# Moving the transposition and the broadcast of the attention maxima later in a block of queries

## The chip, the core and the metric

The kernel runs on one core of a Trainium2 chip. The core has a matrix engine (TensorE, PE in the profile; its weight loads are PEld), a vector engine (VectorE, DVE), a scalar engine (ScalarE, ACT), a general engine (GpSimd, POOL) and an engine that only issues transfers (SyncE, SP). They run side by side, each through its own list of instructions in a fixed order, and wait for one another by semaphores. The metric is the device time of one execution in microseconds (us). Everything is computed in float32.

## What is computed

Four layers run over `x` of shape 4 x 64 x 64 x 128 (four images of 4096 positions with 128 channels). Layer 0 is attention over 7 x 7 neighbourhoods. Layer 1, in which the change lies, is full attention of every position over all 4096 positions of its image:

```python
h = group_norm(x, gn_scale, gn_bias)
hf = h.reshape(B, N, C)                      # N = 4096, C = 128
q = hf @ wq + bq
k = hf @ wk + bk
v = hf @ wv + bv
w_ = jnp.einsum('bqd,bkd->bqk', q, k) * C ** (-0.5)
w_ = jax.nn.softmax(w_, axis=2)
o = jnp.einsum('bqk,bkd->bqd', w_, v)
o = o @ wo + bo
return x + o.reshape(B, H, W, C)
```

Layer 2 is a gated linear layer with a layer norm, four tiles of 128 positions at a time. Layer 3 is a selective scan with a depthwise 3 x 3 convolution ahead of it.

## The kernel before

The kernel goes image by image (`b` of 4). For each image `layer_1` works through 32 blocks of 128 queries, `i`. A block's scores against the 4096 keys are computed with the keys on the partitions: 32 tiles of 128 keys, four of which make a group (`G = 4`, eight groups, `g`). The softmax of a block is spread over three turns of the loop, so that TensorE always has products of two blocks to mix:

- In turn `i` (`score`, L607 to L620), each group is four products into one PSUM tile (L613, `sc`). ScalarE copies the tile into `st` in SBUF (L616), which holds all 32 tiles of scores. VectorE keeps an elementwise maximum over the key tiles in `mx`: one instruction after group 3 (L618) and one each after groups 5 and 7 (L620).
- At the start of turn `i + 1`, `fold` (L622 to L625) halves `mx` three times, to one maximum per partition of keys and per query. During that turn `soften` (L627 to L640) finishes the maximum and takes the exponential. TensorE transposes the 128 x 128 maxima (L630, `pt`), VectorE reduces them to one negative maximum per query (L632, `nm`) and spreads these on a diagonal (L634, `dm`), and TensorE multiplies the diagonal by ones (L636, `pb`), which brings each query's maximum to all partitions. VectorE adds `pb` to the scores in two halves (L639), and ScalarE takes the exponential of each half in place (L640).
- In turn `i + 2`, `value` (L642 to L646) multiplies each key tile of exponentials by the values; a column of ones beside the values gives the sum. `finish` (L648 to L651) divides and adds to `x`, which lies in `xt`.

Within a turn the program says, for each group: soften the block before if it is its place, then four scores of block `i`, then four value products of block `i - 2`. `soften` has its place ahead of the scores of group 2; after the last block, where there are no scores, at group 0.

After each turn `between(i)` does a piece of other work: a step of layer 2 for the positions that are done, and a piece of the front of layer 3 (`front`) for positions that went through layer 2. Layer 2 has four steps, one per turn, in a cycle of four: `turn` (transposes, L275, and a sum, L689), `mix` (L695 to L710), `add` (L717 to L727) and `norm` (four normalising instructions on VectorE, L734, a transposition and L742). The front of layer 3 puts in projections (L786, L814), the convolution's taps (L828, L843 and L847 on ScalarE, L855 and L858 on GpSimd, L864 on VectorE), activations (L806) and small products (L914, L919, L935, L940, L947).

The program order isn't the order on the engines. A scheduler decides, ahead of the run, the order of each engine's list: it goes by the program order as a priority and by its own estimate of when each instruction is ready, and it may let an instruction stand behind later ones of the program. The semaphores follow from the order. Only a few instructions are kept in program order explicitly (L806 among them).

Buffers around the change: four PSUM tiles are shared by the scores and the products of layers 2 and 3 (tag "s"), two by `pt`, `pb` and other transpositions (tag "t"), two by `po` and others (tag "o"). `st` is in a ring of five large SBUF tiles, `mx1` and `dm1` have two buffers each, `nm1` three.

Of the kernel before, what the change touches and what calls it, by code (L numbers as in the profile page):

```python
# [22 lines left out]
F32 = mybir.dt.float32  # L23
AF = mybir.ActivationFunctionType
ALU = mybir.AluOpType
# [4 lines left out]
P = 128  # L30
B, H, W, C = 4, 64, 64, 128
L = H * W
NT = L // P
# [105 lines left out]
def layers_0_to_2(  # L139
    ctx, tc, xf, mata, matb, rows, rpb, convw, sel, ident, cl, dram, big, ring, early, x3_d, ub_d, zf_d, y_d, dbl_d, ct_d, gw_d, bw_d  # L140
):
    nc = tc.nc
    wp = ctx.enter_context(tc.tile_pool(name="wa", bufs=1))
    tmp = ctx.enter_context(tc.tile_pool(name="tmp", bufs=2))
# [8 lines left out]
    def ps_t(shape, name):  # L153
        return psp.tile(shape, F32, name=name, tag="t", bufs=2)
# [90 lines left out]
    ones = wp.tile([P, P], F32, name="ones")  # L245
# [308 lines left out]
    def layer_1(b, xt, hT, st, between):  # L554
# [49 lines left out]
        def start(i):  # L604
            k = Block()
            k.st = ring([P, NT, P], "st")
            k.mx = tmp.tile([P, 2 * G, P], F32, name="mx1", tag="mx1")  # L607
            return k

        def score(i, k, g):  # L610
            ps = ps_s([P, G, P], "sc1")
            for r in range(G):
                nc.tensor.matmul(  # L613
                    ps[:, r, :], lhsT=kT[:, bass.ts(G * g + r, P)], rhs=qT[:, bass.ts(i, P)], start=True, stop=True
                )
            nc.scalar.copy(k.st[:, G * g:G * g + G, :], ps)  # L616
            if g == 3:
                nc.vector.tensor_tensor(k.mx, k.st[:, 0:8, :], k.st[:, 8:16, :], ALU.max)  # L618
            elif g in (5, 7):
                nc.vector.tensor_tensor(k.mx, k.mx, k.st[:, 4 * g - 4:4 * g + 4, :], ALU.max)  # L620

        def fold(k):  # L622
            mx = k.mx
            for n in (4, 2, 1):
                nc.vector.tensor_tensor(mx[:, 0:n, :], mx[:, 0:n, :], mx[:, n:2 * n, :], ALU.max)  # L625

        def soften(k):  # L627
            mx = k.mx
            pt = ps_t([P, P], "pt1")
            nc.tensor.transpose(pt, mx[:, 0, :], ident)  # L630
            nm = sml.tile([P, 1], F32, name="nm1", tag="nm1")
            nc.vector.tensor_reduce(nm, pt, AX.X, ALU.max, negate=True)  # L632
            dm = tmp.tile([P, P], F32, name="dm1", tag="dm1")
            nc.vector.tensor_scalar(dm, ident, nm, None, ALU.mult)  # L634
            pb = ps_t([P, P], "pb1")
            nc.tensor.matmul(pb, lhsT=ones, rhs=dm, start=True, stop=True)  # L636
            for h in range(2):
                part = k.st[:, 16 * h:16 * h + 16, :]
                nc.vector.tensor_tensor(part, part, pb.unsqueeze(1).to_broadcast([P, 16, P]), ALU.add)  # L639
                nc.scalar.activation(part, part, AF.Exp)  # L640

        def value(k, g):  # L642
            if g == 0:
                k.po = ps_o([P, C + 1], "po1")
            for j in range(G * g, G * g + G):
                nc.tensor.matmul(k.po, lhsT=k.st[:, j, :], rhs=v[:, j, :], start=(j == 0), stop=(j == NT - 1))  # L646

        def finish(i, k):  # L648
            ri = sml.tile([P, 1], F32, name="ri1", tag="ri1")
            nc.vector.reciprocal(ri, k.po[:, C:C + 1])  # L650
            nc.vector.scalar_tensor_tensor(xt[:, i, :], k.po[:, 0:C], ri, xt[:, i, :], ALU.mult, ALU.add)  # L651

        blocks = {}
        for i in range(NT + 2):
            if 0 < i <= NT:
                fold(blocks[i - 1])
            if i < NT:
                blocks[i] = start(i)
            for g in range(NT // G):

                if 0 < i <= NT and g == (2 if i < NT else 0):
                    soften(blocks[i - 1])
                if i < NT:
                    score(i, blocks[i], g)
                if i >= 2:
                    value(blocks[i - 2], g)
            if i >= 2:
                finish(i - 2, blocks.pop(i - 2))
            between(i)
# [414 lines left out]
    for b in range(B):  # L1084
# [5 lines left out]
        def between(i):  # L1090

            n, part = divmod(i - 6, 4)
            if i == 6 and b + 1 < B:
                ahead.append(load_x(b + 1))
            if i >= 6 and n < NCH:
                parts[part](n)
            first_part(i)
            if b + 1 < B and i == NT + 1:
                edge_of[b + 1] = edge_bias(0)
            if b + 1 < B and i == NT + 3:  # L1100
                bias_m[:] = bias_tiles()
                for t, d in zip(bias_m, bias_d):
                    nc.sync.dma_start(t, d)

        first_part = front(b)
        first_part(-1)
        layer_1(b, xt, *handed.pop(b), between)
        if b + 1 < B:
            coming = layer_0(b + 1, ahead[0], edge_of[b + 1])
# [379 lines left out]
```

## Time and profile before

| | |
|---|---|
| median of 3 runs | 3786.41 us (3785.8 to 3787.2) |
| the profiled execution's own time | 3789.72 us |
| its span on the core | 3787.9 us, 69412 instructions |
| layer 1 of the four images | 248 to 744, 984 to 1526, 1752 to 2290, 2516 to 3067 us of the span |
| busy in these four stretches, 2127 us | PE 2026.6, DVE 1696.2, ACT 1483.9, POOL 474.6 us |

The profile is of one execution. A line of the list of waits names the engine and line that waited, for whom, the total in us, how often, and the longest. In a list in order of time each line has a start, a length in us, the engine, the line of the kernel, the operation, what is written from what with partitions x elements, and how many such instructions stand together. In brackets is how long the engine stood idle before it, and whose signal ended that. One matrix product of the program is recorded as two instructions; so a group of four scores is "x8".

### The profile page before, as it was taken

The numbers are of one execution on the slowest core, as the hardware profiler recorded it, in microseconds if no ns is written. First come the engines' busy times: TensorE is split into PE (matmuls) and PEld (weight loads), VectorE is DVE, ScalarE is ACT, GpSimd is POOL, SyncE is SP. The second block draws the span as 40 slices with busy tenths as digits, with TensorE's granted clock in tenths as the row PEclk, the third lists the DMA queues.
The fourth block names the chain that finished last, engine by engine and source line by source line (L and its number), as shares of the span: only waits on it lengthen the run. The fifth ranks groups of instructions, "written<-read, shape, count | busy, mean of one in ns | idle before, by whom it ended". The sixth has DMA issues, their size and how long they took to land.

```text
span 3787.9 us, 69412 instructions
## 1 busy us (share of the span) xinstructions
PE 3375.8 (89%) x26780; PEld 2780.8 (73%) x26780; DVE 2838.1 (75%) x4865; ACT 2679.2 (71%) x4350; POOL 1421.5 (38%) x1562
## 2 busy tenths in 40 slices
PE   6999999999999999998999999989999987666647
PEld 3779989966789889667998897779988863222236
DVE  2657777766677788666777876767778866999968
ACT  3865667778677776686676777867767657999934
POOL 5500012245122122351212223523222226999866
PEclk8999999999999999999999999999999996555569
DMA  5100000131010012310211113100101158999998
GB/s 139 50 3 26 12 18 29 44 100 35 18 46 29 32 64 89 118 41 12 71 60 64 46 43 97 44 1 26 44 27 62 54 192 207 232 223 206 210 273 287
DMA packets 205199, 319.30 MB, mean 84 GB/s; under 512 B 23583, under 2 KB 112188, under 8 KB 200732
## 3 DMA queue, kind: packets, MB, share of 16 engines
q1 hardware_dynamic: 165572, 237.57, 18.4%
q0 software_dynamic: 19776, 68.56, 9.9%
q10 hardware_dynamic: 19520, 8.73, 0.8%
q8 instruction: 211, 3.46, 0.4%
q14 instruction: 120, 0.98, 0.1%
HBM read 150.91 MB, written 155.56 MB: 81 GB/s over the span
## 4 chain that ended last, share of the span: by engine, by line
PE 54%; DVE 22%; POOL 8%; ACT 7%; issue 6%; DMA 3%; SPq 1%; POOLq 0%; DVEq 0%; ACTq 0%
PE po L646 15%; PE sc L613 15%; DVE mx L625 4%; POOL inp L1216 4%; PE pt L493 4%; DVE acc L864 4%; DVE st L639 3%; DVE mx L620 3%; POOL y L1255 2%; PE po L504 2%; PE sc L458 2%; ACT st L640 2%; ACT st L616 2%; PE pp L514 1%; PE pz L814 1%
## 5 line engine op out<-in xcount | busy, mean ns | idle before, releaser
L646 PE MATMUL po<-v,st 128*128 128x129 f32 x8192 | 1081.6, 275 | 4.1 <-ACT st L640 4.1
L613 PE MATMUL sc<-qT,kT 128*128 128x128 f32 x8192 | 1082.6, 276 | 0.4 <-ACT st L616 0.4
L613 PEld LDWEIGHTS sc<-qT,kT 128*128 128x128 f32 x8192 | 1004.1, 193 | 21.9 <-issue 18.1
L646 PEld LDWEIGHTS po<-v,st 128*128 128x128 f32 x8192 | 999.3, 192 | 5.4 <-issue 5.4
L616 ACT COPY st<-sc 128x512 f32<-128x512 f32 x1024 | 578.7, 584 | 526.8 <-PE sc L613 519.7
L639 DVE TENSOR_TENSOR st<-st,pb 128x2048 f32<-128x2048 f32 x256 | 573.8, 2283 | 48.0 <-PE pb L636 47.4
L620 DVE TENSOR_TENSOR mx<-mx,st 128x1024 f32<-128x1024 f32 x256 | 315.2, 1231 | 239.7 <-ACT st L616 237.7
L640 ACT ACTIVATE st<-st 128x2048 f32<-128x2048 f32 x256 | 483.4, 1908 | 6.3 <-DVE st L639 4.7
L1205 PE MATMUL pdt<-dbl,dt 8*128 8x512 f32 x512 | 307.3, 1080 | 145.1 <-ACT de L1212 145.1
L1216 POOL TENSOR_TENSOR inp<-de,ub 128x1024 f32<-128x1024 f32 x128 | 411.2, 4465 | 35.5 <-DMA dbl_d<-dq 24.9
L1205 PEld LDWEIGHTS pdt<-dbl,dt 8*128 8x128 f32 x512 | 114.1, 312 | 335.4 <-ACT de L1212 273.1
L710 POOL TENSOR_TENSOR x<-x,row 128x512 f32<-128x512 f32 x32 | 49.9, 1560 | 789.6 <-PE pt L275 789.6
L484 POOL TENSOR_SCALAR pr<-pr,sm 128x308 f32<-128x308 f32 (+3 forms) x512 | 244.2, 498 | 220.4 <-DVE sm L482 190.3
L855 POOL TENSOR_TENSOR gsum<-gsum,tp 128x504 f32<-128x504 f32 (+1 forms) x176 | 253.6, 1443 | 123.3 <-ACT gsum L843 83.9
L476 ACT ACTIVATE pr<-pr,mx 128x308 f32<-128x308 f32 (+3 forms) x512 | 262.5, 517 | 0.0
L625 DVE TENSOR_TENSOR mx<-mx 128x512 f32<-128x512 f32 (+2 forms) x384 | 256.8, 669 | 6.1
L462 DVE CUSTOM_DVE_ANT_0 pr<-sc,bias_m 128x266 f32<-128x266 f32 (+1 forms) x384 | 152.0, 452 | 112.4 <-PE sc L458 104.5
L1240 DVE TENSOR_TENSOR_SCAN h<-h,end,inp 128x1024 f32<-128x1024 f32 x96 | 221.1, 2346 | 15.7 <-POOL inp L1216 7.8
L493 PE MATMUL pt<-ident,pr 128*88 128x128 f32 (+5 forms) x1472 | 204.4, 276 | 7.8 <-ACT prT L495 7.8
L1255 POOL DMA_DIRECT2D y<-yo x112 | 205.9, 2809 | 7.6 <-DVE yo L1254 4.0
L864 DVE SCALAR_TENSOR_TENSOR acc<-xh,cc,acc 128x512 f32<-128x512 f32 (+3 forms) x244 | 197.2, 835 | 3.8 <-ACT acc L828 2.7
L493 PEld LDWEIGHTS pt<-ident,pr 128*88 128x88 f32 (+5 forms) x1472 | 164.2, 138 | 44.9 <-ACT prT L495 31.6
(233 smaller groups left out, 5234.5 us busy)
## 6 DMA issues: line engine op xcount, KB each, us to landing
y<-yo POOLq DMA_DIRECT2D x112, 512.0 KB, 10.7
y<-du SPq DMA_DIRECT2D x160, 256.0 KB
zf_d<-zf SPq DMA_DIRECT2D x64, 256.0 KB
ub_d<-u SPq DMA_DIRECT2D x64, 256.0 KB
ub<-ub_d SPq DMA_DIRECT2D x16, 1024.0 KB
yl<-y SPq DMA_DIRECT2D x64, 256.0 KB
zc<-zf_d SPq DMA_DIRECT2D x64, 256.0 KB
x<-in_x SPq DMA_DIRECT2D x128, 64.0 KB
```

Source lines behind the costliest of these rows:

```text
L493: pin(nc.tensor.transpose(pt[0:n, h, :], k.pr[:, h, at:at + n], ident))
L613: nc.tensor.matmul(ps[:, r, :], lhsT=kT[:, bass.ts(G * g + r, P)], rhs=qT[:, bass.ts(i, P)], start=True, stop=True)
L616: nc.scalar.copy(k.st[:, G * g:G * g + G, :], ps)
L620: nc.vector.tensor_tensor(k.mx, k.mx, k.st[:, 4 * g - 4:4 * g + 4, :], ALU.max)
L625: nc.vector.tensor_tensor(mx[:, 0:n, :], mx[:, 0:n, :], mx[:, n:2 * n, :], ALU.max)
L639: nc.vector.tensor_tensor(part, part, pb.unsqueeze(1).to_broadcast([P, 16, P]), ALU.add)
L640: nc.scalar.activation(part, part, AF.Exp)
L646: nc.tensor.matmul(k.po, lhsT=k.st[:, j, :], rhs=v[:, j, :], start=(j == 0), stop=(j == NT - 1))
L864: nc.vector.scalar_tensor_tensor(acc, x, c, acc, ALU.mult, ALU.add)
L1205: nc.tensor.matmul(pdt[j][:, g, :], lhsT=dt[o:o + RANK, P * f:P * f + P], rhs=at(dbl[o:o + RANK, :], k & 2, g0, g0 + CH), start=True, stop ...
L1216: nc.gpsimd.tensor_tensor(by_rows(inp), by_rows(de), at(ub_s[f], b ^ (k & 1), SC * n, SC * n + SC), ALU.mult)
L1255: nc.gpsimd.dma_start(here if f == 1 and k == 3 else there, yo, accum_op=ALU.add)
```

## The change

`soften` is cut in two. The new `turn_maxima` has the transposition, the reduction and the diagonal; `soften` keeps the product with ones, the adds and the exponentials. `turn_maxima` has its place ahead of the scores of group 3, and `soften` ahead of the scores of group 4. After the last block both are at group 0, one behind the other. The diagonal is handed over in the block (`k.dm`). No instruction is added, dropped or resized. From L627 on the lines of the changed kernel are shifted by one to four.

```diff
-        def soften(k):
-            mx = k.mx
+        def turn_maxima(k):
             pt = ps_t([P, P], "pt1")
-            nc.tensor.transpose(pt, mx[:, 0, :], ident)
+            nc.tensor.transpose(pt, k.mx[:, 0, :], ident)
             nm = sml.tile([P, 1], F32, name="nm1", tag="nm1")
             nc.vector.tensor_reduce(nm, pt, AX.X, ALU.max, negate=True)
-            dm = tmp.tile([P, P], F32, name="dm1", tag="dm1")
-            nc.vector.tensor_scalar(dm, ident, nm, None, ALU.mult)
+            k.dm = tmp.tile([P, P], F32, name="dm1", tag="dm1")
+            nc.vector.tensor_scalar(k.dm, ident, nm, None, ALU.mult)
+
+        def soften(k):
             pb = ps_t([P, P], "pb1")
-            nc.tensor.matmul(pb, lhsT=ones, rhs=dm, start=True, stop=True)
+            nc.tensor.matmul(pb, lhsT=ones, rhs=k.dm, start=True, stop=True)
             for h in range(2):
                 part = k.st[:, 16 * h:16 * h + 16, :]
                 nc.vector.tensor_tensor(part, part, pb.unsqueeze(1).to_broadcast([P, 16, P]), ALU.add)
...
             for g in range(NT // G):
 
-                if 0 < i <= NT and g == (2 if i < NT else 0):
+
+                if 0 < i <= NT and g == (3 if i < NT else 0):
+                    turn_maxima(blocks[i - 1])
+                if 0 < i <= NT and g == (4 if i < NT else 0):
                     soften(blocks[i - 1])
                 if i < NT:
                     score(i, blocks[i], g)
```

## The prediction

> **What bounds the kernel now.** I read the page first (busy time, chain), then the list of waits, then the lines in order of time inside layer 1, engine by engine.
>
> ```profile
> PE 3375.8 (89%) x26780; PEld 2780.8 (73%) x26780; DVE 2838.1 (75%) x4865; ACT 2679.2 (71%) x4350; POOL 1421.5 (38%) x1562
> PE 54%; DVE 22%; POOL 8%; ACT 7%; issue 6%; DMA 3%; SPq 1%; POOLq 0%; DVEq 0%; ACTq 0%
> ```
>
> TensorE is the bound of layer 1, but VectorE holds a fifth of the chain. Where it holds TensorE, the waits say (engine and line, for whom, us in total, times, longest):
>
> ```profile
> DVE mx L620 <- ACT st L616: 237.7, 174, 3.3
> DVE nm L632 <- PE pt L630: 119.5, 106, 3.9
> PE pt L630 <- DVE mx L625: 74.0, 61, 3.7
> PE pb L636 <- DVE dm L634: 17.8, 15, 3.1
> ```
>
> TensorE stands 74.0 us at the transposition and about 18.7 at the product (17.8, and 0.9 for others): 92 us of 3787.9 is the most that this change can take away there. One period of four blocks of queries, in order of time (start, us, what; idle before it in brackets): first TensorE, then VectorE, ScalarE and GpSimd.
>
> ```profile
> 2612.94 0.33 PE L630 MATMUL pt<-ident,mx 128*128 128x128 f32 x1 [1.38 <-DVE mx L625]
> 2631.66 0.27 PE L630 MATMUL pt<-ident,mx 128*128 128x128 f32 x1
> 2650.79 0.33 PE L630 MATMUL pt<-ident,mx 128*128 128x128 f32 x1 [0.88 <-DVE mx L625]
> 2668.10 0.33 PE L630 MATMUL pt<-ident,mx 128*128 128x128 f32 x1 [1.64 <-DVE mx L625]
> 2684.89 0.33 PE L630 MATMUL pt<-ident,mx 128*128 128x128 f32 x1 [1.37 <-DVE mx L625]
> ...
> 2677.56 1.06 PE L613 MATMUL sc<-qT,kT 128*128 128x128 f32 x8
> ```
>
> ```profile
> 2631.97 0.29 DVE L632 TENSOR_REDUCE nm<-pt 128x1 f32<-128x128 f32 x1 [3.88 <-PE pt L630]
> 2652.14 2.46 DVE L734 TENSOR_SCALAR x<-x,mv,rd 128x128 f32<-128x128 f32 x2
> 2654.53 4.47 DVE L639 TENSOR_TENSOR st<-st,pb 128x2048 f32<-128x2048 f32 x2
> 2660.06 0.59 DVE L734 TENSOR_SCALAR x<-x,mv,rd 128x128 f32<-128x128 f32 x2
> 2679.27 1.23 DVE L620 TENSOR_TENSOR mx<-mx,st 128x1024 f32<-128x1024 f32 x1 [1.24 <-ACT st L616]
> 2680.53 1.65 DVE L625 TENSOR_TENSOR mx<-mx 128x512 f32<-128x512 f32 x1
> 2682.96 1.88 DVE L625 TENSOR_TENSOR mx<-mx 128x256 f32<-128x256 f32 x2
> ```
>
> ```profile
> 2674.39 1.91 ACT L640 ACTIVATE st<-st 128x2048 f32<-128x2048 f32 x1
> 2678.66 0.59 ACT L616 COPY st<-sc 128x512 f32<-128x512 f32 x1 [1.20 <-PE sc L613]
> ```
>
> ```profile
> 2652.01 1.27 POOL L858 TENSOR_TENSOR acc<-acc,gsum 128x512 f32<-128x512 f32 x1
> 2681.59 4.44 POOL L855 TENSOR_TENSOR gsum<-gsum,tp 128x504 f32<-128x504 f32 x3
> ```
>
> The reader is to see that the wait depends on what layer 2 and the front of layer 3 put into the block. I call a block by its step of layer 2: turn (L689), mix (L705), add (L719), norm (L734, L742). Summed over the lines like those above, the transposition waits 26.9 us behind 28 turn blocks, 0 behind 24 mix, 29.2 behind 24 add, 14.9 behind 24 norm, 2.2 elsewhere. In a turn block the copy of the last scores is on time (score at 2677.56, copy at 2678.66), and the folds are slow (3.5 us for what takes 1.47 elsewhere) while GpSimd adds; in an add block VectorE is busy without a gap. The product waits 4.6 us in norm blocks, 10.7 in the first blocks of images 2 to 4, 3.4 in mix.
>
> **The change part by part.** No instruction is added or removed, and the moved step issues no DMA. The built program shows what the scheduler makes of it.
>
> *TensorE.* Before: two groups, transposition, scores of group 2, product. After: three groups, transposition, scores and values of group 3, product. A group (four scores, four values) takes 2 x 0.893 = 1.79 us (2675.78, 2676.67, 2677.56). The transposition stands 1.79 us later; the product stands 1.95 after it (0.16 + 1.79) instead of 1.1.
>
> *VectorE.* In 111 of 121 blocks the first maximum of the new scores (L618), which stood behind the two adds of L639, now stands between dm and the adds; before it did in 5. It needs the copy of group 3. From the transposition at 0: score 0.16, copy 1.25 to 1.84, L618 1.9 to 3.1, adds 3.1 to 7.5 (before 1.9 to 6.3). Behind the adds queue the exponentials: ScalarE's order is now copies 0 to 5, exponential, copy 6, exponential, copy 7 (before: 0 to 3, exponential, 4, exponential, 5, 6, 7). So exponential 5.7 to 7.6, copy 6 to 8.1, exponential to 9.9, copy 7 to 10.4, though its scores are there at 8.7. The shift of 1.79 is thus mostly eaten: last L620 10.4 to 11.6, L689 0.6, folds 3.5 as in the row: 15.7. TensorE arrives at 16 x 0.893 + 0.16 + 0.30 + 0.44 (product, L275) = 15.2. Turn blocks keep about 0.6 of 1.37. Eighteen of the 28 waits are above 1.2; 18 x 0.6 = 10.8 stays of 26.9: **16 us gained**. With folds at 1.47 all of it goes (27); with three slow folds of 1.4 nothing. I take the row of this same place.
>
> *Add blocks.* VectorE runs without a gap from nm to the fold. Two of its eight L864 (0.70 each) now stand at the end of the mix block, in the 3.88 us that VectorE idles there. So a wait falls by 1.4: the eight above 2 us (20.5 together) keep 9.3; the 0.9 and below go, except in three cycles where copy 3 comes late (3 L847 and L843 before it) and L618 idles about 1.3: about 13 of 29.2 stays, **16 gained** (bounds 0 and 29).
>
> *Norm blocks.* Nothing of L734 stands in them behind dm any more, and VectorE is done 1 us before TensorE: **15 gained** (14.9). In the first blocks of images 2 to 4 one or two L864 leave nm and dm: 6 of 12.9 gained.
>
> *What takes the place of the waits.* In 18 of the 24 cycles all four L734 (and L727) now stand at the end of the add block, ahead of the next nm. So nm, dm and the product wait for them, and behind the product all of TensorE. From the fold's end: TensorE's product stands at 0.16 + 1.95 = 2.1; VectorE has it ready at 0.15 + S + 0.76 (nm 2668.47 to product 2669.23), S the four L734. The stall is S - 1.2. S is 3.05 in the cycle shown (2.46 while GpSimd adds, 0.59 free) and 1.28 in the cycles where GpSimd is idle, 4 of the 18: 14 x 1.85 + 4 x 0.1 = 26 us, against the 4.6 it replaces: **22 lost**. Bounds: S = 1.28 always (1.8 us in all) and S = 4 x 1.43, the longest L734 of the trace (18 x 4.5 = 81). I take 3.05, since GpSimd's three adds and L858 fall into the same stretch as before.
>
> ```profile
> L734 DVE TENSOR_SCALAR x<-x,mv,rd x128: 329/341/1431, 371.8 to 3110.0; 128x128 f32<-128x128 f32 x128
> ```
>
> [...]
>
> **Sum.** 16 + 16 + 15 + 6 - 22 = 31 us. The profiled execution took 3789.7 (span 3787.9 and 1.8 around), 3.3 above the median of the three runs: 3789.7 - 31 = 3758.7, or 3755 to 3756 against the median of 3786.4.
>
> **Rivals.** *All of it goes.* GpSimd's adds start earlier and L734 runs free: S = 1.28, the loss of 22 becomes a gain of 3: 56 us, 3730; if the folds are free too, up to the 92: 3694. For it: 4 of 18 cycles are so already. Against: GpSimd's work is released by the same copies (L787) as before.
>
> *Nothing net.* S near 4.4 cancels the gains: 53 + 4.6 = 18 x (S - 1.2). One image 1 block shows 4.91 for four L734. 3779 to 3794.
>
> *Slower.* The L734 ahead of nm meet GpSimd at every instance: S between 4.9 and 5.7, a stall of 3.7 to 4.5 in 18 norm blocks, 67 to 81 us against 58: 3796 to 3810. It decides from S = 4.4. [...] Against: the second pair in the row above took 0.59.
>
> **How the numbers follow.** Forecast (3740 to 3772) 0.42; all of it 0.20; nothing net 0.12; slower 0.26. Faster by over 0.2% (7.6 us, about what a measurement tells from no change) 0.62, within 0.12, slower 0.26. The range leaves out some 0.05 below and 0.1 above: 3712 to 3806; the forecast's own is 3740 to 3772.
>
> **What would show it.** TensorE's wait at the transposition falls from 74 to 20-35 us; its wait at the product rises from 18 to 30-45, in norm blocks; L618 starts 1.9 behind the transposition, L639 3.1; copy 7 stands directly behind the second exponential. I am wrong if L639 starts earlier than 3 behind the transposition, if the value products wait for L640, or if the product does not wait in norm blocks.

## The result and the profile after

The changed kernel takes 3785.06 us (median of 12 runs, 3780.5 to 3789.3). The kernel before took 3788.36 us in the 12 runs beside it. The ratio is 0.9991, with a 95% interval of 0.9984 to 0.9999: some 3 us faster, which is within the 0.2% that count as no change. The forecast was a gain of 31 us. The profiled execution of the changed kernel took 3781.34 us (span 3779.6).

The page of the changed kernel, busy time and the chain by engine:

```profile
PE 3371.0 (89%) x26780; PEld 2773.0 (73%) x26780; DVE 2895.9 (77%) x4865; ACT 2668.6 (71%) x4350; POOL 1434.7 (38%) x1562
PE 58%; DVE 19%; ACT 8%; POOL 6%; issue 5%; DMA 2%; SPq 1%; POOLq 0%; DVEq 0%; ACTq 0%
```

The same work keeps VectorE busy for 58 us longer than before (2838.1). Nothing was added to it, so its instructions take longer. The list of waits of the changed kernel (who waits, for whom, us, times, longest; here the transposition is L629, the product L637, dm L633):

```profile
PE pb L637 <- DVE dm L633: 50.9, 23, 4.3
PE pt L629 <- DVE mx L625: 40.4, 38, 2.2
DVE mx L618 <- ACT st L616: 77.5, 80, 3.5
DVE acc L868 <- ACT acc L832: 49.4, 21, 3.7
```

TensorE's wait at the transposition fell from 74.0 to 40.4 us, and its wait at the product rose from 17.8 to 50.9. The two together were 91.8 us and are 91.3: the change exchanged one wait for the other.

Where this happens shows in a sum over the blocks of the four images, each from its transposition to the next, by the block's step of layer 2. Waits at the transposition are booked to the block that they end. The slow clock is each block's length times what its mean granted clock lacks to 1; the view gives the clock to two decimals, so sums of it are good to some 0.5 us.

```
block (how many)   length, us        wait at transposition   wait at product   slow clock
                   before   after    before  after           before  after     before  after
turn (28)          456.4    454.1    26.9    26.9             0.0     0.0       0.0     0.0
mix (28)           512.3    504.1     0.7     0.0             3.4     4.3       1.6     1.8
add (24)           461.2    451.8    29.2     8.8             0.0     5.9       0.6     0.0
norm (24)          400.9    416.0    14.9     2.9             4.6    32.4      11.2    13.7
others (20)        307.7    308.5     2.2     2.2            10.7     8.3       0.0     0.0
sum               2138.6   2134.6
```

Turn blocks kept all of their wait and gained 2.3 us, norm blocks lost 15 us, and add and mix blocks gained 18.

**A turn block of the changed kernel**, in order of time (its transposition stood at 1134.89). VectorE first, then ScalarE's second exponential and the copy of the last scores, GpSimd, and TensorE's next transposition:

```profile
1136.71 1.23 DVE L618 TENSOR_TENSOR mx<-st 128x1024 f32<-128x1024 f32 x1 [0.90 <-ACT st L616]
1137.86 4.48 DVE L640 TENSOR_TENSOR st<-st,pb 128x2048 f32<-128x2048 f32 x2
1145.08 2.12 DVE L620 TENSOR_TENSOR mx<-mx,st 128x1024 f32<-128x1024 f32 x1 [0.17 <-ACT st L616]
1147.72 3.81 DVE L625 TENSOR_TENSOR mx<-mx 128x512 f32<-128x512 f32 x3
...
1142.65 1.92 ACT L641 ACTIVATE st<-st 128x2048 f32<-128x2048 f32 x1
1144.47 0.58 ACT L616 COPY st<-sc 128x512 f32<-128x512 f32 x1
...
1144.85 1.27 POOL L714 TENSOR_TENSOR x<-x,row 128x512 f32<-128x512 f32 x1 [25.83 <-PE pt L275]
1146.24 5.14 POOL L859 TENSOR_TENSOR gsum<-gsum,tp 128x504 f32<-128x504 f32 x3
...
1151.58 0.33 PE L629 MATMUL pt<-ident,mx 128*128 128x128 f32 x1 [1.46 <-DVE mx L625]
```

The order is as forecast: the first maximum (L618) at 1.82 us behind the transposition, the adds (L640) at 2.97, the last copy directly behind the second exponential. But the last maximum (L620 at 1145.08) starts 0.23 us after GpSimd's L714, and takes 2.12 us where its like takes 1.22. In the kernel before, in the block at 2668.10 that the prediction shows, it started at 2679.27, ahead of GpSimd's L710, and took 1.23:

```profile
2680.03 1.60 POOL L710 TENSOR_TENSOR x<-x,row 128x512 f32<-128x512 f32 x1 [24.28 <-PE pt L275]
```

So it loses 0.9 now, and the folds take 3.81.

**A norm block of the changed kernel**, VectorE, then GpSimd, then TensorE:

```profile
1115.48 3.88 DVE L738 TENSOR_SCALAR x<-x,mv,rd 128x128 f32<-128x128 f32 x4
1119.28 0.28 DVE L631 TENSOR_REDUCE nm<-pt 128x1 f32<-128x128 f32 x1
1119.59 0.29 DVE L633 TENSOR_SCALAR dm<-ident,nm 128x128 f32<-128x128 f32 x1
...
1115.28 1.27 POOL L862 TENSOR_TENSOR acc<-acc,gsum 128x512 f32<-128x512 f32 x1
1116.51 2.50 POOL L951 TENSOR_TENSOR u<-u,bb 128x512 f32<-128x512 f32 x2
...
1120.02 0.46 PE L637 MATMUL pb<-dm,ones 128*128 128x128 f32 x2 [2.50 <-DVE dm L633]
1120.32 1.30 PE L613 MATMUL sc<-qT,kT 128*128 128x128 f32 x8
1121.41 1.93 PE L647 MATMUL po<-v,st 128*128 128x129 f32 x8
1123.13 1.67 PE L613 MATMUL sc<-qT,kT 128*128 128x128 f32 x8
1124.63 1.06 PE L647 MATMUL po<-v,st 128*128 128x129 f32 x8
```

All four normalising instructions (L738) stand ahead of nm in 18 of the 24 norm blocks, as forecast. In six of these 18 they take 1.11 us and the product does not wait; in all, it waits in 13 of the 24 blocks, mostly 2.4 to 2.6 us. In the block shown they take 3.88 us; the forecast took 3.05. And the wait costs more than itself: the groups behind it take 1.93 and 1.67 us in place of 1.06. The windows view gives the granted clock (window, length, busy time of PE, PEld, DVE, ACT, POOL with counts, then the clock, DMA share and GB/s):

```profile
1120.00:1121.00 1.00, 0.98 (x9) 1.00 (x10) 1.00 (x2) 0.00 (x0) 0.00 (x0) 0.99 0.58 217
1121.00:1122.00 1.00, 1.00 (x7) 1.00 (x6) 1.00 (x2) 0.35 (x1) 0.00 (x0) 0.50 0.08 16
1122.00:1123.00 1.00, 1.00 (x7) 1.00 (x6) 1.00 (x1) 0.85 (x2) 0.00 (x0) 0.50 0.00 0
1123.00:1124.00 1.00, 1.00 (x7) 1.00 (x7) 1.00 (x2) 0.00 (x0) 0.00 (x0) 0.50 0.00 0
1124.00:1125.00 1.00, 1.00 (x9) 1.00 (x9) 1.00 (x1) 0.17 (x1) 0.00 (x0) 0.80 0.00 0
```

The half clock begins 1 us behind the stall, at 1120.99, and lasts 3.41 us: this block takes 19.48 us, and a norm block with the same stall and no slow stretch takes 17.84.

### The profile page after: what moved, and what is told of

The parts are those of the page before. It is cut to its first block, busy times and chain, and to the rows that moved or that the text cites. A ratio compares the mean times of both kernels' runs of the same rounds, so it can differ in the third digit from the quotient of the medians.

```text
span 3779.6 us, 69303 instructions
## 1 busy us (share of the span) xinstructions
PE 3371.0 (89%) x26780; PEld 2773.0 (73%) x26780; DVE 2895.9 (77%) x4865; ACT 2668.6 (71%) x4350; POOL 1434.7 (38%) x1562
## 4 chain that ended last, share of the span: by engine, by line
PE 58%; DVE 19%; ACT 8%; POOL 6%; issue 5%; DMA 2%; SPq 1%; POOLq 0%; DVEq 0%; ACTq 0%
PE sc L613 17%; PE po L647 17%; PE pt L493 4%; DVE mx L625 4%; POOL inp L1220 3%; ACT st L641 3%; DVE acc L868 3%; PE sc L458 3%; PE po L504 2%; DVE mx L620 2%; POOL y L1259 2%; DVE x L738 2%; DVE h L1244 1%; PE pp L514 1%; DVE st L640 1%
## 5 line engine op out<-in xcount | busy, mean ns | idle before, releaser
L640 DVE TENSOR_TENSOR st<-st,pb 128x2048 f32<-128x2048 f32 x256 | 574.0, 2280 | 7.8 <-PE pb L637 7.7
L641 ACT ACTIVATE st<-st 128x2048 f32<-128x2048 f32 x256 | 484.1, 1911 | 15.3 <-DVE st L640 14.4
L1220 POOL TENSOR_TENSOR inp<-de,ub 128x1024 f32<-128x1024 f32 x128 | 412.7, 4491 | 36.6 <-DMA ub_d<-u 32.7
L620 DVE TENSOR_TENSOR mx<-mx,st 128x1024 f32<-128x1024 f32 x256 | 337.9, 1320 | 43.9 <-ACT st L616 40.7
L714 POOL TENSOR_TENSOR x<-x,row 128x512 f32<-128x512 f32 x32 | 40.8, 1274 | 762.1 <-PE pt L275 762.1
L859 POOL TENSOR_TENSOR gsum<-gsum,tp 128x504 f32<-128x504 f32 (+1 forms) x176 | 267.9, 1524 | 129.3 <-ACT gsum L847 83.2
L868 DVE SCALAR_TENSOR_TENSOR acc<-xh,cc,acc 128x512 f32<-128x512 f32 (+3 forms) x244 | 204.5, 845 | 49.9 <-ACT acc L832 49.4
L618 DVE TENSOR_TENSOR mx<-st 128x1024 f32<-128x1024 f32 x128 | 163.2, 1275 | 77.5 <-ACT st L616 77.5
```

What stands on the lines that cost most here:

```text
L868: nc.vector.scalar_tensor_tensor(acc, x, c, acc, ALU.mult, ALU.add)
L1220: nc.gpsimd.tensor_tensor(by_rows(inp), by_rows(de), at(ub_s[f], b ^ (k & 1), SC * n, SC * n + SC), ALU.mult)
```

## The experiments

All times are medians, each beside runs of the kernel before on the same chip (3787.2 to 3788.4 us). The columns give the waits in layer 1 as in the table above, and the slow clock summed over all blocks.

```
kernel         us        ratio (95% interval)      transposition        product  slow
                                                   turn   add    norm   norm     clock
before         3788.36                             26.9   29.2   14.9    4.6     13.4
after          3785.06   0.9991 (0.9984-0.9999)    26.9    8.8    2.9   32.4     15.5
m1_behind      3755.75   0.9911 (0.9894-0.9928)     5.3    6.0    0.0   35.0     26.0
norm_behind    3741.05   0.9875 (0.9861-0.9890)    26.9    8.8    0.4    0.0      6.9
both_behind    3701.67   0.9770 (0.9756-0.9785)     5.4    6.0    2.1    0.0      3.4
no_pool_adds   3668.07   one run                    0.0    0.0    0.5    0.4      0.0
before_norm    3768.24   0.9945 (0.9932-0.9959)    26.9   29.2    0.4    3.7     10.0
half_norms     3765.96   0.9940 (0.9922-0.9958)    27.0    8.8    0.0   17.8     12.3
pd_whole       3798.14   1.0025 (1.0013-1.0037)    26.9   14.4    3.6   42.3     29.4
best           3700.51   0.9767 (0.9754-0.9780)     5.4    6.0    2.1    0.0      3.5
whole_at_3     3766.19   0.9941 (0.9925-0.9958)     0.0    3.7    0.0   40.7     27.9
split_2_3      3783.24   0.9989 (0.9980-0.9999)    28.7   36.6   10.9    3.5      8.4
both_whole_3   3708.64   0.9792 (0.9778-0.9807)     0.0    4.3    0.0   10.8      3.6
```

### The first maximum behind the adds (m1_behind)

```diff
-            if g == 3:
-                nc.vector.tensor_tensor(k.mx, k.st[:, 0:8, :], k.st[:, 8:16, :], ALU.max)
-            elif g in (5, 7):
+            if g in (5, 7):
...
+        def first_max(k):
+            tc.keep_in_program_order(nc.vector.tensor_tensor(k.mx, k.st[:, 0:8, :], k.st[:, 8:16, :], ALU.max))
...
                     soften(blocks[i - 1])
+                if i < NT and g == 4:
+                    first_max(blocks[i])
```

> The changed kernel with one more move: the first maximum of a block (the two halves of the first 16 tiles of scores) stands behind the two adds on VectorE's list in every block, and not ahead of them. Theory A (order): in the changed kernel this 1.23 us instruction runs between dm and the adds, so adds, exponentials, the copy of the eighth group, the last maximum and the folds all start about 1.1 us late, and in the turn blocks that eats the group that the transposition was moved back by. Then the 27 us of waits at the transposition behind the 28 turn blocks fall below 12, and the time is 13 to 20 us under the changed kernel's 3785. [...]

The turn blocks' waits fell to 5.3 us and the time by 29 us, more than theory A asked. The turn blocks are 22.6 us shorter than in the changed kernel (431.5 against 454.1), nearly all of it wait. The same place in this kernel (the transposition stood at 1131.85; the first maximum is L621 here, the last L618, the adds L641, the folds L626):

```profile
1134.17 4.48 DVE L641 TENSOR_TENSOR st<-st,pb 128x2048 f32<-128x2048 f32 x2 [1.40 <-PE pb L638]
1138.58 1.22 DVE L621 TENSOR_TENSOR mx<-st 128x1024 f32<-128x1024 f32 x1
1141.79 1.22 DVE L618 TENSOR_TENSOR mx<-mx,st 128x1024 f32<-128x1024 f32 x1
1143.52 3.84 DVE L626 TENSOR_TENSOR mx<-mx 128x512 f32<-128x512 f32 x3
...
1141.80 2.34 POOL L717 TENSOR_TENSOR x<-x,row 128x512 f32<-128x512 f32 x1 [25.06 <-PE pt L275]
...
1147.41 0.33 PE L630 MATMUL pt<-ident,mx 128*128 128x128 f32 x1 [0.33 <-DVE mx L626]
```

How it comes about is not what theory A said. The adds start 0.65 us earlier in the block, but the last maximum only 0.25 us earlier: 9.94 us behind the transposition, against 10.19. That is enough to be 0.01 us ahead of GpSimd's instruction instead of 0.23 us behind it. Now GpSimd is the one that is held (2.34 us instead of 1.27), and the maximum takes its 1.22. The sum, 0.25 + 0.90 = 1.15, is the fall of the wait from 1.46 to 0.33. The folds are as slow as before. So the order and the meeting with GpSimd act together: the order decides who comes first, and here the second of the two took 0.9 to 1.1 us longer.

Of the rest, the add blocks are 13.8 us shorter, only 2.8 of it wait; TensorE's busy time in them falls by 10.7, to which pd_whole returns. The norm blocks became 8.3 us longer: their slow clock rose from 13.7 to 22.6.

### The normalising behind the adds (norm_behind)

`norm` is cut: its four normalising instructions are a function `scale`, called through `behind(i)`.

```diff
                     soften(blocks[i - 1])
+                    behind(i)
...
-        def norm(n):
+        def scale(n, pin=True):
             mv, rd = kept.pop(n)
             for k in range(4):
                 x = xt[:, 4 * n + k, :]
-                nc.vector.tensor_scalar(x, x, mv[:, k, 0:1], rd[:, k:k + 1], ALU.subtract, ALU.mult)
+                ins = nc.vector.tensor_scalar(x, x, mv[:, k, 0:1], rd[:, k:k + 1], ALU.subtract, ALU.mult)
+                if pin:
+                    tc.keep_in_program_order(ins)
+
+        def norm(n):
+            if n in kept:
+                scale(n, False)
...
+        def behind(i):
+            n, part = divmod(i - 6, 4)
+            if i >= 6 and part == 3 and i < NT:
+                parts[4](n)
```

> The changed kernel with the four normalising instructions of layer 2 kept behind the two adds of a block, and not ahead of the reduction nm, in the 24 steps that lie inside a layer 1 loop. Theory A (what stands in front of nm): the product's waits in the norm blocks fall from 32 us to 4 or less, nothing takes their place, and the time is 25 to 30 us under the changed kernel's 3785, about 3757. Theory B (the work only moves): the four instructions, 1.3 to 3.9 us, now delay the maxima and folds of the same block, and 1 to 2 us a block come back as a wait at the next transposition; then the time is within 8 us of the changed kernel's, and the waits at the transposition behind norm blocks rise from 3 us to 20 or more.

Theory A holds, and the gain is 44 us where it asked for 25 to 30. The four (L739 here) stand behind the adds, run at full speed there, and the product (L637) follows without a wait:

```profile
1108.59 0.53 DVE L633 TENSOR_SCALAR dm<-ident,nm 128x128 f32<-128x128 f32 x1
1111.28 4.47 DVE L640 TENSOR_TENSOR st<-st,pb 128x2048 f32<-128x2048 f32 x2
1115.68 1.10 DVE L739 TENSOR_SCALAR x<-x,mv,rd 128x128 f32<-128x128 f32 x4
...
1109.85 0.39 PE L637 MATMUL pb<-dm,ones 128*128 128x128 f32 x2
```

The norm blocks fall from 416.0 to 368.6 us. Of these 47.4 us, 32.4 are the product's waits, 2.5 waits at the transposition, and 10.4 the slow clock (13.7 to 3.3). The expectation had left out the clock.

### Both moves (both_behind)

The edit is the two diffs above together.

> Both of the moves: the first maximum behind the adds, and the four normalising instructions behind the adds in the norm blocks. If both theories of order hold and do not meet, the gains add: 3785 less 28 less 16 is about 3741. If the waits in the turn blocks belong to GpSimd's adds, about 3757 is left. If the two moved pieces together (1.2 and 1.3 to 3.9 us) now push the second and third maxima of a norm block back, the waits at the transposition behind norm blocks come back with 1 to 2 us each, and the time is 3765 or more.

3701.67 us, 2.3% below the kernel before. The measured single gains (29.3 and 44.0 us) add up to 3711.8; of the 10 us more, 8.3 are what the norm blocks had lost in m1_behind, by its size to the slow clock (8.9 us more there), which follows on the stall that norm_behind takes away.

### Without GpSimd's adds of the taps (no_pool_adds)

```diff
-                nc.gpsimd.tensor_tensor(a, a, p, ALU.add)
                 if k == len(of) - 1:
-                    acc = accs[n & 1][:, f, :]
-                    nc.gpsimd.tensor_tensor(acc, acc, sums.pop((n, f)), ALU.add)
+                    sums.pop((n, f))
```

> The changed kernel without GpSimd's adds of the taps (the products of four of the nine taps are made by ScalarE but never added), which leaves that part of the convolution out. Everything on VectorE, ScalarE and TensorE stays in its place. [...] Theory A (order alone): the normalising instructions become shorter and the product's waits go, but the turn blocks keep 15 us or more of their waits, and the time is 3750 to 3760.

Every wait at the transposition and almost every wait at the product is gone, and the layer 1 blocks are 117.9 us shorter (2016.7). Theory A, by which the turn blocks keep 15 us of their waits, fails. In 18 of the 24 cycles the four normalising instructions take 1.11 us. In the turn blocks, though, the last maximum still comes second to GpSimd (2.12 us): the instruction that it meets, L714, is an addition of layer 2 and not of the taps, and it stayed. What became free are the folds, 1.46 us in place of 3.81 (the transposition stood at 1109.52):

```profile
1119.71 2.12 DVE L620 TENSOR_TENSOR mx<-mx,st 128x1024 f32<-128x1024 f32 x1 [0.17 <-ACT st L616]
1122.35 1.46 DVE L625 TENSOR_TENSOR mx<-mx 128x512 f32<-128x512 f32 x3
...
1119.47 1.28 POOL L714 TENSOR_TENSOR x<-x,row 128x512 f32<-128x512 f32 x1 [22.19 <-PE pt L275]
```

With m1_behind this says: the turn blocks' wait of 1.46 us needs both, a maximum that comes second to L714 and folds that meet GpSimd's adds of the taps. Freeing the folds alone ends the wait, and freeing the maximum alone leaves 0.33 us of it. This single run has no interval, but its effect is far above the spread of any kernel here.

### The kernel before, with the normalising behind the adds (before_norm)

The diff is that of norm_behind, on the kernel before the change.

> The kernel before the change, with layer 2's four normalising instructions kept behind the two adds, as in norm_behind. It asks whether the change itself is worth anything once these are out of the way (norm_behind, which has both, took 3741). Theory A (the change buys back waits at the transposition, and the normalising instructions hid it): the turn and add blocks here keep their waits of 27 and 29 us, only the 15 us of waits behind the norm blocks and their 8 slow clock stretches go, so the time is 3760 to 3775, and the change is worth 20 to 30 us on top of it. Theory B (all of the gain of norm_behind is the moved normalising, the change is worth nothing): the time is within 6 us of 3741.

3768.24 us: theory A. The turn and add blocks keep their waits to a tenth of a microsecond. So with the normalising out of the way the change is worth 27 us (3768.2 to 3741.1). The forecast without its two terms of the norm blocks is 16 + 16 + 6 = 38. Alone the change is worth 3. With the first maximum behind the adds as well it is worth 67 us (3768.2 to 3701.7 of both_behind), since in the kernel before the first maximum stands ahead of the adds in only 5 of 124 blocks.

### Two of the four ahead of nm (half_norms)

`scale` takes only `k` = 2 and 3 behind the adds, and `norm` keeps the other two.

```diff
-            for k in range(4):
+            for k in (2, 3) if pin else range(4):
+                if (n, k) in done:
+                    continue
```

> The changed kernel with two of the four normalising instructions of a step kept behind the adds and two left ahead of nm. Theory A (stall is what stands ahead of nm, less a cover of about 1.4 us, and a stall under 2 us costs no clock): four take 3.9 us and stall 2.5, so two take 1.9 us and stall 0.5 to 0.6 us in 13 blocks, the product's waits in the norm blocks come to 5 to 10 us in place of 32, the slow clock stretches of 13.7 us in these blocks fall to 4 or less, and the time is 3743 to 3755. Theory B (the loss is in proportion to the instructions): the waits are about 16 us, half of the slow stretches stay, and the time is about 3763.

The waits came to 17.8 us, near theory B's 16, and the time to 3766: theory A's formula fails. The slow clock in the norm blocks fell to 5.1 us, close to what A asked, but the add blocks, which had none, now have three slow stretches (5.1 us) behind waits of 1.95 us that they had in the changed kernel too; the last section shows how the two differ. VectorE, GpSimd and the product in the same block as above (the normalising is L743 here):

```profile
1115.32 2.40 DVE L743 TENSOR_SCALAR x<-x,mv,rd 128x128 f32<-128x128 f32 x2
1117.64 0.28 DVE L631 TENSOR_REDUCE nm<-pt 128x1 f32<-128x128 f32 x1
1117.96 0.99 DVE L633 TENSOR_SCALAR dm<-ident,nm 128x128 f32<-128x128 f32 x1
...
1115.13 1.27 POOL L874 TENSOR_TENSOR acc<-acc,gsum 128x512 f32<-128x512 f32 x1
1116.36 2.51 POOL L963 TENSOR_TENSOR u<-u,bb 128x512 f32<-128x512 f32 x2
...
1119.09 0.46 PE L637 MATMUL pb<-dm,ones 128*128 128x128 f32 x2 [1.72 <-DVE dm L633]
```

GpSimd runs three instructions of 1.25 us without a gap, to 1118.87. Each normalising instruction takes 1.2 us beside them, and now dm falls into the same run: 0.99 in place of 0.29, ending as GpSimd ends. By these rows the wait goes by the end of GpSimd's run and by how many instructions must get through before it, dm among them; a fixed price for an instruction and a fixed cover don't describe it.

### The narrow products kept together (pd_whole)

In the changed kernel the scheduler put two of the sixteen narrow products of `lower` (pd, L918) between the two projections pi (L790) of the next positions, in 17 steps:

```profile
1318.38 1.02 PE L790 MATMUL pi<-xc,win 128*128 128x512 f32 x2
1319.33 0.41 PE L918 MATMUL pd<-u,wx 128*32 128x128 f32 x2
1319.67 1.12 PE L790 MATMUL pi<-xc,win 128*128 128x512 f32 x2
1320.72 0.64 PE L918 MATMUL pd<-u,wx 128*32 128x128 f32 x14
1321.29 1.16 PE L613 MATMUL sc<-qT,kT 128*128 128x128 f32 x8
```

That is 2.91 us from the first pi to the scores; whole it is 2.39 in the kernel before.

```diff
-                    nc.tensor.matmul(
+                    tc.keep_in_program_order(nc.tensor.matmul(
                         pd[HD * g:HD * g + HD, :], lhsT=wx[:, f, :], rhs=u[f][:, bass.ts(g, P)],
                         start=(f == 0), stop=(f == 1),
-                    )
+                    ))
```

> The changed kernel with the sixteen narrow products (128x32 weights, tile pd) of a step of layer 3 kept together on TensorE's list. In the changed kernel the scheduler set the first two of them between the two products pi of the same step in 17 steps, and there the group took 2.91 us from the first pi to the next scores, against 2.39 us where it is whole. Theory A (a switch between wide and narrow products costs 0.26 us, and these steps have two switches more): the time falls by 0.52 times 17, about 9 us, to 3776. Theory B (the difference is hidden by a later wait, or is the matmul's modelled end): no change, within 3 us of 3785.

Neither theory: 3798.14 us, slower by 10 against the kernel before, with a spread of 3783.7 to 3806.5 over ten runs. TensorE's busy time in the add blocks does fall, from 437.0 to 431.2 us. The add blocks stay as long (451.8 and 451.5), because the wait at the transposition behind them rises by the same 5.6 us: VectorE ends those blocks. And now some norm blocks meet GpSimd that had not. In the block at 1259 the normalising starts 0.11 us before a GpSimd add (L859) and takes 4.12 us. The changed kernel had all four through in 1.12 us before that add began:

```profile
1259.39 4.12 DVE L738 TENSOR_SCALAR x<-x,mv,rd 128x128 f32<-128x128 f32 x4
1263.43 0.28 DVE L631 TENSOR_REDUCE nm<-pt 128x1 f32<-128x128 f32 x1
...
1259.50 1.36 POOL L859 TENSOR_TENSOR gsum<-gsum,tp 128x504 f32<-128x504 f32 x1 [0.84 <-ACT tp L851]
```

### All three moves (best)

The edits of both_behind and pd_whole together.

> All three moves on the changed kernel: the first maximum behind the adds, the four normalising instructions behind the adds, and the sixteen narrow products kept together. With the first two the narrow products were already whole in most steps (split in 9, at 0.3 to 0.5 us each), so theory A of the narrow products expects 3 to 4 us below the 3702 of both_behind, about 3698; theory B expects 3702.

3700.51 us, against 3701.67 for both_behind: no difference that these runs can tell, as theory B has it.

### The transposition's move alone (whole_at_3)

```diff
-                if 0 < i <= NT and g == (4 if i < NT else 0):
+                if 0 < i <= NT and g == (3 if i < NT else 0):
                     soften(blocks[i - 1])
```

> One part of the change alone: the transposition goes from behind the second to behind the third group of scores, but the product stays directly behind the scores of that group, as before the change (no group of scores and values between them). Here the scheduler leaves the first maximum behind the adds in all but 5 of 128 blocks. Theory A (the move buys the turn and add blocks, the first maximum was what lost them): the waits at the transposition behind turn blocks fall from 27 us below 6 and behind add blocks below 9; without the cover the product waits some 1 us more wherever something stands ahead of dm: 40 to 50 us in the norm blocks, and about 0.3 us in the others (8 to 13 us in mix and add). Sum against before: gains of 21, 20 and 12, losses of 40 and of no cover: 3765 to 3785. Theory B (the turn blocks' wait goes with the position, not with the first maximum): 20 us or more of it stay, and the time is above 3790.

Theory A: the turn blocks' 26.9 us go to 0 and the add blocks' 29.2 to 3.7, while the product's waits in norm blocks rise to 40.7 and the slow clock there to 24.4. Moving the transposition alone gains 21 us on the kernel before. The position is worth what was hoped; the second half of the change, with the first maximum that it drew ahead of the adds, took the turn blocks' share back.

### The product's move alone (split_2_3)

```diff
-                if 0 < i <= NT and g == (3 if i < NT else 0):
+                if 0 < i <= NT and g == (2 if i < NT else 0):
                     turn_maxima(blocks[i - 1])
-                if 0 < i <= NT and g == (4 if i < NT else 0):
+                if 0 < i <= NT and g == (3 if i < NT else 0):
                     soften(blocks[i - 1])
```

> The other part alone: the transposition stays behind the second group of scores, and the product goes one group back, behind the third. The first maximum stays behind the adds in all but 6 blocks. The waits at the transposition stay as before the change or grow, since adds and exponentials come up to 0.9 us later at their earliest (turn 27 to 40, add 29 to 45). The product's waits: the mix and add blocks gain 8 to 13 us of small waits. What stands ahead of nm decides the norm blocks as in the changed kernel. Theory A (the product's place is worth little by itself): 3785 to 3800. Theory B (the cover alone brings the gain): under 3775.

3783.24 us, 4 below the kernel before, a little under theory A's range. The waits at the transposition went as A said (turn 28.7, add 36.6). The norm blocks did not go as in the changed kernel: the product waits 3.5 us there and not 32.4, and in 21 of the 24 none of the four normalising instructions stands ahead of nm. In whole_at_3, which moves the transposition too, at least one does in 20. So it is the later place of the transposition that lets them slip ahead, and not that of the product. The first maximum needs both moves: it stands ahead of the adds in 6 blocks here, in 8 of whole_at_3 and in 111 of the 124 of the changed kernel.

### Both moves, and the product one group earlier (both_whole_3)

The edits of both_behind, with `soften` at group 3.

> both_behind (3702) with the product directly behind the scores of the third group, in place of one group later. Adds start up to 0.9 us earlier, so the 18 waits of 0.33 us at the transposition behind turn blocks and the 1 us waits behind three add blocks go (about 9 us). The cover of the product is 0.9 us and not 1.8. Theory A (the second group of cover is worth more than it costs): small waits of 0.2 to 0.4 us at the product in most of the 121 blocks, 20 to 30 us, and the time is 3710 to 3725. Theory B (with nothing ahead of nm the product needs no second group): 3690 to 3700.

3708.64 us, just under theory A's range and clearly above B's. The turn blocks lose their last 5 us of wait, but the product waits 10.8 us in the norm blocks, mostly 0.6 to 0.8 at a time; small waits in most blocks, which theory A named, did not come. The second group of cover is worth 7 us net.

## Why the prediction was wrong

The sum was 31 us, the measured gain 3.3, in the profile's layer 1 blocks 4.0. Term by term:

- **Turn blocks, 16 us: wrong.** Nothing of the wait went. The step that failed is the one that put the last maximum at "10.4 to 11.6", one free instruction of 1.2 us, and the slow folds behind it. The times of L618, of the adds and of the copy were right to 0.2 us (the last maximum started at 10.19), but GpSimd's L714 starts at 9.96, a meeting that the working did not look for, and the maximum came second: 2.12 us. The folds took 3.81 and not 3.5. So the block's folds end 16.6 us behind the transposition and not 15.7, and the wait is 1.46 and not 0.6. m1_behind shows that 0.25 us decides who comes first, no_pool_adds that the slow folds are the other half, and whole_at_3 that the place of the transposition is not the cause.
- **Add blocks, 16 us: the waits right, the blocks not.** 20.4 us of wait went. But 5.9 us came at the product in three blocks where taps (L868) that wait for ScalarE stand between nm and dm, which the working did not look for. And the scheduler tore the narrow products apart, worth 5.8 us of TensorE's time in these blocks by pd_whole. 9.4 us were left.
- **Norm blocks, 15 us gained at the transposition: near.** 12.0.
- **The product's new wait, 22 us net lost: too small, and without its consequence.** 27.8 us net (4.6 to 32.4). In the cycle shown the four took 3.88 us and not the 3.05 of the row that was chosen: in the row before the change two of the four ran free, behind the adds, and ahead of nm all four fall into GpSimd's run, at 0.97 us each on average (3.88 / 4). The stall itself was less than S - 1.2 (2.50 at 3.88), so the two errors partly cancelled.
- **The slow clock: missing altogether.** norm_behind shows its size: 10.4 us of the 47.4 that the norm blocks gained there are slow clock. In the comparison of before and after it is only 2.5 us, because the long waits at the transposition had cost it as well: of the eight above 2 us in the kernel before (2.18 to 3.68), seven have a slow stretch at or behind them, and the change took five of the eight away.
- **First blocks of images, 6 us: wrong.** 2.4 us of wait, and these blocks are 0.8 us longer.
- **Mix blocks, 0: wrong in our favour.** 8.2 us. Before the change the product started 1.36 us behind the transposition in most of these blocks, where 1.12 was the shortest, with a gap too small to be listed as a wait; most mix blocks are 0.37 us shorter now (18.71 to 18.34).

The sum of the measured blocks is 2.3 + 8.2 + 9.4 - 15.1 - 0.8 = 4.0. The case that came is the second rival, "nothing net", in its time, but by luck and not by its mechanism: it needed S near 4.4, and S was 3.9 in ten of the 18 blocks and 1.1 in six, while the turn blocks' waits gave nothing.

Two of the forecast's signs failed: the wait at the transposition fell to 40.4 us and not to 20 to 35, and the wait at the product rose to 50.9 and not to 30 to 45. What it said would refute it did not clearly occur: the product waits in norm blocks, the value products' waits for the exponentials only grew from 4.1 to 6.6 us, and the adds at 2.97 stand at the edge of the 3 that it named. It asked whether the moved instructions stand where they should, and they did. It did not ask whether the last maximum and GpSimd still meet in the same order.

## What to carry to other kernels

When a step moves, look at what the scheduler lets slip in front of the instructions that release the critical engine: here a 1.2 us maximum ahead of the adds and four normalising instructions ahead of nm cost nearly all that the move won, and two fixed places in the order turned 0.1% into 2.3%. Where VectorE and GpSimd met here, an end depended on who came first: 0.01 us ahead of GpSimd the last maximum took 1.22 us, 0.23 us behind it 2.12. Give such a term both values in the range, not the one of the present row. And price a stall of TensorE by its length plus the slow clock that came with it here in some blocks, 1.9 us on average where there was any (below).

## What the runs showed of the hardware

- **Stretches at half the clock (0.50 granted) stood at waits of TensorE of about 2 us and more, but not at all of them, and the place of the wait in time told which.** Over the profiles of the kernels that compute everything (twelve, with before, after and best; the layer 1 blocks alone), each block's longest wait at its transposition or product was set beside its granted clock. Under 1.8 us none of 1316 blocks had a slow stretch. From 1.8 to 2.1 us 5 of 27 had one, to 2.4 us 19 of 54, to 2.8 us 25 of 51, and above that 36 of 40. A block's slow clock, where it had any, came to 1.9 us on average. Of two norm blocks of the changed kernel with waits of 2.49 and 2.48 us, one has a slow stretch and the other has none. The traces show where they differ. In these twelve, all 164 slow stretches between 248 and 3070 us of the span begin on a grid of 3.413 us, to within 0.005 us: those of the changed kernel at 1120.99 and 1332.61, for one, lie 62 steps apart. Of the 172 waits of 1.8 us and more, 79 have at least 1.96 us inside one step of the grid, and every one of these blocks has a slow stretch; of the 82 with less than 1.90 us inside any one step, two have one; of the 11 between, four. The wait of 2.49 us, which ends at 1884.58, has 2.42 inside one step; the one of 2.48, which ends at 2098.29, has 1.39. The waits of 1.95 us in the add blocks lie within one step in half_norms; in the changed kernel a step has 1.74 to 1.79 of them.
- **Instructions of VectorE and GpSimd took longer beside each other, and where the last maximum met GpSimd's add of layer 2, the one that started second did.** In the changed kernel a maximum that takes 1.22 us elsewhere took 2.12 when it started 0.23 us behind the add; in m1_behind the add took 2.34 in place of 1.27 when it started 0.01 us behind the maximum. Normalising instructions of 0.28 us each (1.11 for four) took 0.97 each on average beside GpSimd's run in the changed kernel (3.88 for four) and 1.2 in half_norms (2.40 for two). The folds took 3.81 us beside GpSimd's adds of the taps and 1.46 in no_pool_adds.
- **Narrow products between wide ones came with more time on TensorE.** With two narrow products set between two wide ones, the group of four pi and sixteen pd instructions was 0.52 us longer (2.91 against 2.39), in all 17 such steps and at full clock.
